# Per-slot amounts of filler, and their pace within a slot, in a convolution and attention kernel on Trainium2

## The chip, the cores and the metric

The kernel runs on one core of one Trainium2 chip. The core has a matrix engine (TensorE, PE in the profile), a vector engine (VectorE, DVE), a scalar engine (ScalarE, ACT), a general one (GpSimd, POOL), and a queue for transfers (SyncE, SP). Each engine works through its own instructions in order; semaphores hold an instruction until what it needs is there. Time is the device time of one execution in microseconds, the median of several.

## What is computed

Eight images of 512 channels by 32 x 32 pixels, all in float32, go through two layers. The first is a group norm, then a block with two bottleneck attentions; the second is a group norm, then a 1 x 1 convolution with a masked and permuted weight matrix. Cut to what matters:

```python
# layer 0, on gn(x): 32 groups
t = silu(bn(conv1x1(gn(x), cv1_w)))              # 512 -> 512
ys = [t[:, :256], t[:, 256:]]
for i in range(2):                               # two blocks
    z = silu(bn(conv3x3(ys[-1], m_cv1_w[i])))    # 256 -> 256
    q, k, v = split(conv1x1(z, m_qkv_w[i]))      # 4 heads of 64
    logits = einsum('bhdi,bhdj->bhij', q, k + r_i) * 64 ** -0.5
    z = einsum('bhij,bhdj->bhdi', softmax(logits), v)
    z = silu(bn(conv1x1(z, m_cv2_w[i])))
    ys.append(ys[-1] + z)
x = x + silu(bn(conv1x1(concat(ys), cv2_w)))     # 1024 -> 512
# layer 1
x = x + conv1x1(gn(x), w_eff)                    # 512 -> 512, w_eff from conv, S, T
```

## The kernel before

**Slots and units.** The attention of one image in one block is a slot; there are 16. In groups of two images the order is (image p, block 0), (p+1, 0), (p, 1), (p+1, 1). Slots are numbered s = 0 to 15, and k below counts groups, so that slot 4k is the first of a group. A slot has four units (`Unit`, line 493): two pairs of heads by two halves of the 1024 queries, pair by pair. The two heads of a pair run side by side in the matrix engine.

**What a unit does.** The keys are cut into eight tiles, taken two at a time in four steps, t = 0, 2, 4, 6. At the start `top` (line 524) transposes the running maxima (tile mt) and VectorE reduces them (nm); `spread` (533) brings the negated maxima back over the partitions (mb). Then in each step, on its engines: `soften` (VectorE adds mb to the stored logits st), `exponent` (ScalarE takes exp of st in place, GpSimd adds it to the sum), `values` (TensorE: po from st and v, for the two tiles before), and `logits` of the **next** unit (TensorE: lg from q and k; ScalarE copies lg to st; VectorE takes the maximum mx). In the step t = 0 come also `finish` and `divide` of the unit before (the denominators den, a reciprocal rb, and q overwritten by po times rb). Four pairs of lists (`pe_turn`, `act_turn`, `in_turn`) fix the order of these instructions on their engines. The order of everything else follows from the order in which the kernel issues it; the framework that compiles the program may move an instruction up where the one ahead of it would wait.

**Filler.** All other work on TensorE is laid between the steps as filler, as Python generators that yield a planned cost in microseconds after each piece (called planner us below). A piece of a 1 x 1 convolution is two matmuls and counts 1.72, a piece of the 3 x 3 convolution (`conv3`, Winograd products) three matmuls and 1.33, a piece of values' projection eight matmuls and 0.89. In the profile each float32 matmul of the program is two instructions.

**What is needed in a slot** is what the next slot's attention wants: `conv3` of the next slot's image (six products of four pieces, 31.9), `project` (q, k and v; per pair of heads four pieces of 1.72 and two of 0.89, 17.3 in sum, planned as 21), and where images come to their second block `conv_m2` (four pieces, planned as 7). After a block-1 slot `conv_m2(1)` of its image is needed too, and then `finishing` puts four items on the background list.

**The background list** (`Background`, line 849) holds work that no attention waits for soon: `First` (normalisation and first convolution of half an image; four groups of two pieces, 13.76 in all), `Second` (the convolution over the concatenation; four groups of four pieces, 27.5) and `Last` (layer 1; four groups of two pieces, 13.76). A group ends in an evacuation: SiLU on ScalarE for First and Second, an addition on VectorE for Last. An item's loads are issued when the item ahead of it begins, and it has a planned time from which it is ready. At the start the list holds eleven First items (the twelfth is held back); `finishing` adds two Second items, the item held back and one Last item, 82.6 in all, and holds another Last item. `take(us)` (line 867) runs pieces up to that amount, to the end of a group, and what it runs over is taken off the next `take`. Where the list is empty it returns, and where the next item isn't ready it returns, or, with `wait=True`, lets planner time pass without work.

**A slot's filler** (`slot_filler`, line 912) is a list of takes in this order: 8 from the list; for a next slot of block 1, conv_m2(0), then 9 from the list; conv3 (after a block-1 slot: 16 pieces of it, then conv_m2(1) and `finishing`, then the rest of it); 7 from the list; project; where the slot after the next is of block 0, the load of its y and the eight VectorE operations that transform it for conv3, timed by the planner's clock from 8.0 on and 3.3 apart. The sum of the planned amounts is `needed`: 68 in slot 0, 84 in slots 4k+1 and 4k+2, 75 in slots 4k+3 and in slots 4k from 4 on. Behind it comes the rest, the share (`SHARE`) less `needed`, from the list; in slot 15 the rest is 70. `total` is the sum of both.

**The pace** is set by `advance` (line 1041). A slot has 40 equal steps, ten a unit. In unit j it is called at 10j + 0.7 (before top), + 1.4 (before spread), + 2 (before the step t = 0), and then after each of the steps at + 4, + 6, + 8 and + 10. It runs filler until the planned amount reaches a goal, the larger of two terms: the share of the slot times `total`, and a term that completes `needed` at a certain share of the slot. The next slot's first logits are those that the fourth unit issues in its step t = 0, right after the call at step 32 (a share of 0.80). When the slot ends, what is left of its filler is run.

**Ahead and behind.** Before slot 0 the first two images are normalised and convolved, the weights of the 3 x 3 convolutions and of layer 1 are prepared, and the first unit's logits are taken among four takes of 6.8 after one of 7. After slot 15 come the last divisions, conv_m2(1) of the last image, its Second items and the last two Last items.

Of the kernel before, what the change touches and what calls it, by code (L numbers as in the profile page):

```python
# [39 lines left out]
def conv_preact_kernel(ctx: ExitStack, tc: tile.TileContext, x, cv1, cv2, mcv1, qkv, mcv2, bn, rw, rh, conv, s_in, t_in, out):  # L40
# [859 lines left out]
    def call(f, *a):  # L900
        f(*a)
        return
        yield

    def finishing(im):


        bg.add(Second(im, 0), Second(im, 1), held.pop(), Last(im, 0))
        held.append(Last(im, 1))
        bg.prepare()  # L910

    def slot_filler(s):

        prev = slots[s - 1] if s else (None, 0)
        nxt = slots[s + 1] if s + 1 < len(slots) else (None, 0)
        todo, needed = [], 0.0

        def add(us, g):
            nonlocal needed
            todo.append((us, g))  # L920
            needed += us

        im, i = nxt
        add(8.0, bg.take(8.0))
        if im and i == 1:
            add(7.0, im.conv_m2(0))
            add(0.0, call(im.transform, 1, 2.0, 3.3))
            add(9.0, bg.take(9.0))
        products = im.conv3(i) if im else iter(())
        if prev[1] == 1:  # L930
            if im:
                add(21.3, (us for _, us in zip(range(16), products)))
            add(7.0, prev[0].conv_m2(1))
            add(0.0, call(lambda: finishing(prev[0])))
        if im:
            add(10.7 if prev[1] == 1 else 32.0, products)
            add(7.0, bg.take(7.0))
        if im:
            add(21.0, im.project(i))
        if s + 2 < len(slots) and slots[s + 2][1] == 0:  # L940
            add(0.0, call(slots[s + 2][0].load_y))
            add(0.0, call(slots[s + 2][0].transform, 0, 8.0, 3.3))
        rest = SHARE - needed if im else 70.0
        if rest > 0:
            todo.append((rest, bg.take(rest, wait=True)))
        total = sum(c for c, _ in todo)
        return needed, total, todo

    SHARE = 103.0


    small_parameters()
# [71 lines left out]
    before = None  # L1024
    for s in range(len(slots)):
        needed, total, todo = slot_filler(s)
        state = {"done": 0.0}

        def filler():
            for us, g in todo:  # L1030
                start = state["done"]
                for cost in g:
                    clock.tick(cost)
                    state["done"] += cost
                    yield

                state["done"] = max(state["done"], start + us)

        fill = filler()

        def advance(share):
            goal = max(share * total, min(1.0, share / 0.74) * needed + 0.1)
            while state["done"] < goal:
                if next(fill, "end") == "end":
                    break

        steps = 4 * (KT + 2)
        for j in range(4):
            u = units[4 * s + j]
            nxt = units[4 * s + j + 1] if 4 * s + j + 1 < len(units) else None  # L1050
            base = j * (KT + 2)

            advance((base + 0.7) / steps)
            u.top()
            clock.tick(0.9)
            advance((base + 1.4) / steps)
            u.spread()
            clock.tick(0.9)
            advance((base + 2) / steps)
            for t in range(0, KT, 2):  # L1060
                if before and t == 0:
                    before.finish()
                    clock.tick(0.9)
                u.soften(t)
                u.soften(t + 1)
                if t:
                    u.exponent(t)

                lag = u if t else before
                if lag:  # L1070
                    lag.values((t - 2) % KT)
                    lag.values((t - 1) % KT)
                    clock.tick(2.0)
                if before and t == 0:
                    before.divide(0)
                    before.divide(1)
                if nxt:
                    nxt.logits(t)
                    nxt.logits(t + 1)
                    clock.tick(2.0)  # L1080

                if not t:
                    u.exponent(t)
                u.exponent(t + 1)
                advance((base + 4 + t) / steps)
            before = u
        for _ in fill:
            pass
# [6 lines left out]
    im = images[NB - 1]  # L1095
# [55 lines left out]
```

## Time and profile before

| what | value |
|---|---|
| median of 3 runs | 3153.09 us (3151.32 to 3154.78) |
| the profiled execution | 3162.82 us, its span 3161.1 us, mean granted TensorE clock 0.996 |
| TensorE busy, matmuls | 3077.0 us, 97% of the span |
| VectorE, ScalarE, GpSimd busy | 2049.9 us (65%), 1721.0 us (54%), 1398.4 us (44%) |
| slot 0 begins (first transposes of its first unit) | 212.3 us |
| slots 1, 2, 3, 4 begin | 398.3, 579.2, 747.0, 926.5 us |
| slots 14 and 15 begin, the last unit begins | 2698.0, 2877.2, 2993.9 us |
| transfers | 399.35 MB, 126 GB/s over the span |

"Busy" is time in which at least one instruction of an engine runs. A line of groups gives the source line, the engine, the operation, tiles out<-in, shapes, a count, then busy time and the mean of one, and the idle time of the engine just before, with what ended it. A line of the windows view gives a stretch in microseconds from the start, its length, the busy time (and count) of PE, PEld (TensorE's weight loads), DVE, ACT and POOL, the granted clock of TensorE as a part of full speed, and the share and rate of the transfers. A line of the timeline gives start, length, engine, line, operation, tiles, shape and count of a run of like instructions, and in brackets the idle time before it and what ended it. A slot is found in the trace by its transposes mt: each unit begins with eight of them.

### The profile page before, as it was taken

The numbers are of one execution on the slowest core, as the hardware profiler recorded it, in microseconds if no ns is written. First come the engines' busy times: TensorE is split into PE (matmuls) and PEld (weight loads), VectorE is DVE, ScalarE is ACT, GpSimd is POOL, SyncE is SP. The second block draws the span as 40 slices with busy tenths as digits, with TensorE's granted clock in tenths as the row PEclk, the third lists the DMA queues.
The fourth block names the chain that finished last, engine by engine and source line by source line (L and its number), as shares of the span: only waits on it lengthen the run. The fifth ranks groups of instructions, "written<-read, shape, count | busy, mean of one in ns | idle before, by whom it ended". The sixth has DMA issues, their size and how long they took to land.

```text
span 3161.1 us, 34185 instructions
## 1 busy us (share of the span) xinstructions
PE 3077.0 (97%) x11668; PEld 1515.3 (48%) x11668; DVE 2049.9 (65%) x2718; ACT 1721.0 (54%) x2349; POOL 1398.4 (44%) x1867
## 2 busy tenths in 40 slices
PE   7999999998999999999999999999999999999999
PEld 3645354454445454455445454454445454453333
DVE  5446577567667576667666676767666676767642
ACT  3245765855655555644656455544656455546621
POOL 2104444546444554455444454445444464444520
PEclk9999999999999999999999999999999999999999
DMA  8852352421233232424233332424233332413356
GB/s 289 292 182 74 130 180 87 153 77 63 88 116 131 79 128 71 149 84 148 84 116 130 114 127 70 153 85 136 91 110 130 120 120 70 150 64 120 120 205 217
DMA packets 142014, 399.35 MB, mean 126 GB/s; under 512 B 13072, under 2 KB 14352, under 8 KB 141840
## 3 DMA queue, kind: packets, MB, share of 16 engines
q1 hardware_dynamic: 141120, 396.94, 36.6%
q8 instruction: 92, 1.51, 0.2%
q14 instruction: 82, 0.67, 0.1%
q10 hardware_dynamic: 720, 0.23, 0.0%
HBM read 317.42 MB, written 79.69 MB: 126 GB/s over the span
## 4 chain that ended last, share of the span: by engine, by line
PE 75%; DVE 4%; ACT 4%; issue 2%; DMA 1%; POOL 1%; SPq 0%; ACTq 0%; DVEq 0%; POOLq 0%
PE cv L175 15%; PE m L313 13%; PE po L562 12%; PE lg L510 12%; PE l L175 7%; PE qk L175 6%; PE v L405 3%; PE m L175 3%; PE den L576 2%; PE mb L539 2%; PE mt L530 1%; ACT st L517 1%; DVE st L544 1%; ACT st L548 1%; DVE mx L522 1%
## 5 line engine op out<-in xcount | busy, mean ns | idle before, releaser
L555 POOL TENSOR_TENSOR sum<-sum,st 128x256 f32<-128x256 f32 x1536 | 1132.0, 771 | 552.1 <-ACT st L548 547.7
L522 DVE TENSOR_TENSOR mx<-mx,lg 128x512 f32<-128x512 f32 x768 | 477.8, 682 | 417.6 <-ACT st L517 417.4
L517 ACT COPY st<-lg 128x512 f32<-128x512 f32 x1024 | 525.0, 597 | 356.1 <-PE lg L510 331.7
L548 ACT ACTIVATE st<-st 128x1024 f32<-128x1024 f32 x512 | 539.1, 1068 | 304.1 <-DVE st L544 302.9
L544 DVE TENSOR_TENSOR st<-st,mb 128x1024 f32<-128x1024 f32 x512 | 604.4, 1215 | 60.2 <-PE mb L539 60.2
L555 POOL TENSOR_TENSOR sum<-st,st 128x256 f32<-128x256 f32 x256 | 185.1, 754 | 788.8 <-ACT st L548 788.8
L313 PE MATMUL m<-plane,w_m 128*128 128x256 f32 x2304 | 528.8, 383 | 4.9 <-ACT cv2s L130 2.7
L562 PE MATMUL po<-st,v 128*64 128x512 f32 x2048 | 497.8, 605 | 18.2 <-ACT st L548 16.2
L510 PE MATMUL lg<-q,k 64*128 64x512 f32 x2048 | 510.9, 617 | 2.9 <-ACT y L130 2.9
L313 PEld LDWEIGHTS m<-plane,w_m 128*128 128x128 f32 x2304 | 426.4, 189 | 129.5 <-issue 45.1
L175 PE MATMUL cv<-y,w_cv 128*128 128x512 f32 x1024 | 464.5, 599 | 7.9 <-ACT cv2s L130 4.6
L510 PEld LDWEIGHTS lg<-q,k 64*128 64x128 f32 x2048 | 177.3, 186 | 328.2 <-issue 267.4
L175 PEld LDWEIGHTS cv<-y,w_cv 128*128 128x128 f32 x1024 | 185.8, 190 | 248.1 <-issue 226.4
L562 PEld LDWEIGHTS po<-st,v 128*64 128x64 f32 x2048 | 128.8, 136 | 323.6 <-issue 237.3
L175 PE MATMUL cv<-x,w_cv 128*128 128x512 f32 x512 | 237.0, 610 | 10.6 <-ACT y L130 3.7
L175 PE MATMUL l<-x,w_l 128*128 128x512 f32 x512 | 236.9, 606 | 7.9 <-DVE mx L522 6.9
L175 PE MATMUL qk<-z,w_qkv 128*128 128x512 f32 x512 | 234.0, 600 | 1.4 <-DVE mx L522 1.4
L583 DVE RECIPROCAL rb<-rb 128x256 f32<-128x256 f32 x128 | 215.5, 1723 | 26.0 <-ACT rb L579 25.8
L531 DVE TENSOR_REDUCE nm<-mt 128x4 f32<-128x512 f32 x128 | 82.3, 684 | 144.7 <-PE mt L530 144.7
L579 ACT COPY rb<-den 128x512 f32<-128x512 f32 x64 | 37.3, 583 | 230.4 <-PE den L576 230.4
L175 PEld LDWEIGHTS cv<-x,w_cv 128*128 128x128 f32 x512 | 95.3, 194 | 132.0 <-issue 109.3
L175 PEld LDWEIGHTS l<-x,w_l 128*128 128x128 f32 x512 | 93.4, 191 | 130.4 <-issue 112.2
(145 smaller groups left out, 2408.8 us busy)
## 6 DMA issues: line engine op xcount, KB each, us to landing
w_m<-w_m SPq DMA_DIRECT2D x96, 768.0 KB, 4.8
w_cv<-in_cv SPq DMA_DIRECT2D x90, 512.0 KB, 3.5
y<-y SPq DMA_DIRECT2D x64, 512.0 KB, 4.8
x<-in_x SPq DMA_DIRECT2D x56, 512.0 KB, 5.2
y<-y SPq DMA_DIRECT2D x64, 256.0 KB, 3.5
k<-r SPq DMA_DIRECT2D x32, 512.0 KB, 3.6
res<-y SPq DMA_DIRECT2D x32, 512.0 KB, 4.0
xr<-in_x SPq DMA_DIRECT2D x32, 512.0 KB, 4.1
```

The costliest lines, as they stand in the source:

```text
L175: nc.tensor.matmul(ps, w, moving, start=(n == 0), stop=(n == len(terms) - 1))
L313: nc.tensor.matmul(ps[:, ts(co, 256)].rearrange("p (t x) -> p t x", x=F), w[:, co, c, dx], u[:, 9 * c : 9 * c + 8, dx : dx + F], start=(j ...
L405: nc.tensor.matmul(ps[:, ts(j, P)], z[:, c, ts(4 * j4 + j, P)], w[:, c, 512 + P * hp : 512 + P * hp + P], start=(c == 0), stop=(c == IT - 1),)
L510: nc.tensor.matmul(lg[h], self.k[r, ts(t, P)], self.q[r, self.hp, ts(self.half, HALF)], start=True, stop=True)
L517: act_turn(nc.scalar.copy(st[:, h], lg[h]))
L522: in_turn(nc.vector.tensor_tensor(self.mx[:, h], so_far[:, h], lg[h], ALU.max))
L531: nc.vector.tensor_reduce(self.nm[:, h], mt, AX.X, ALU.max, negate=True)
L544: in_turn(nc.vector.tensor_tensor(st, st, flat(self.mb), ALU.add))
L548: act_turn(nc.scalar.activation(st, st, AF.Exp))
L555: nc.gpsimd.tensor_tensor(flat(self.acc)[:, part], flat(so_far)[:, part], st[:, part], ALU.add)
L562: nc.tensor.matmul(self.po[HD * h : HD * h + HD], self.v[:, t, ts(h, HD)], self.st[t][:, h], start=(t == 0), stop=(t == KT - 1),)
L583: nc.vector.reciprocal(self.rb[:, r], self.rb[:, r])
```

## The change

The number SHARE, 103 for every slot, becomes a table: 92 in slot 0, 96 in slot 1, 95 in slots 2 and 14, and 103 in the others. In the pace, the share of the slot at which all needed work is to be done goes from 0.74 to 0.80.

```diff
@@ slot_filler
-        rest = SHARE - needed if im else 70.0
+        rest = SHARE.get(s, 103.0) - needed if im else 70.0
         if rest > 0:
             todo.append((rest, bg.take(rest, wait=True)))
         total = sum(c for c, _ in todo)
         return needed, total, todo
 
-    SHARE = 103.0
+
+    SHARE = {0: 92.0, 1: 96.0, 2: 95.0, 14: 95.0}
@@ advance, in the loop over the slots
         def advance(share):
-            goal = max(share * total, min(1.0, share / 0.74) * needed + 0.1)
+            goal = max(share * total, min(1.0, share / 0.8) * needed + 0.1)
             while state["done"] < goal:
                 if next(fill, "end") == "end":
                     break
```

## The prediction

> **What bounds the kernel now.** I read the page first, for the engine that carries the span, then TensorE's share unit by unit (the windows view, cut at the first transpose of each unit), then the order of instructions where a unit runs short.
>
> ```profile
> span 3161.1 us, 34185 instructions
> PE 3077.0 (97%) x11668; PEld 1515.3 (48%) x11668; DVE 2049.9 (65%) x2718; ACT 1721.0 (54%) x2349; POOL 1398.4 (44%) x1867
> PE   7999999998999999999999999999999999999999
> ...
> PE 75%; DVE 4%; ACT 4%; issue 2%; DMA 1%; POOL 1%; SPq 0%; ACTq 0%; DVEq 0%; POOLq 0%
> ```
>
> TensorE is idle for 3161.1 - 3077.0 = 84 us. The change leaves every matmul in place and reorders filler, so it can win or lose only such idle time, and stretches at a low clock. Some 19 us lie ahead of slot 0 and 13 in the last unit and the tail (windows view, 167.20 - 154.36 = 12.8), which it does not touch. Of the rest, these units have most (columns: stretch, length, then busy time of PE, PEld, DVE, ACT, POOL, the clock, DMA):
>
> ```profile
> 349.50:398.20 48.70, 46.54 (x153) 18.98 (x152) 27.51 (x41) 41.13 (x51) 20.49 (x29) 1.00 0.43 147
> 539.90:579.10 39.20, 38.09 (x133) 15.45 (x132) 24.35 (x34) 32.81 (x41) 19.02 (x27) 1.00 0.26 85
> 718.70:746.90 28.20, 20.40 (x92) 7.41 (x90) 25.01 (x31) 16.63 (x26) 19.09 (x26) 1.00 0.08 29
> 747.00:785.90 38.90, 38.26 (x168) 22.22 (x169) 30.13 (x38) 19.27 (x29) 27.25 (x36) 1.00 0.27 87
> 1422.10:1458.70 36.60, 35.37 (x127) 14.28 (x126) 31.95 (x41) 16.60 (x25) 21.97 (x27) 1.00 0.45 158
> 2840.10:2877.10 37.00, 35.77 (x125) 13.91 (x124) 26.13 (x33) 18.00 (x26) 19.25 (x28) 1.00 0.38 131
> 2877.20:2913.60 36.40, 32.33 (x113) 11.96 (x112) 25.87 (x32) 27.18 (x35) 19.48 (x29) 0.95 0.38 132
> ```
>
> Length less PE: last unit of slot 0 2.16, of slot 1 1.11, **of slot 2 7.80**, first of slot 3 0.64, last of slot 6 1.23, last of slot 14 1.23, **first of slot 15 4.07**. The timeline of TensorE shows why (the bracket is idle time before the group):
>
> ```profile
> 724.02 1.99 PE L510 MATMUL lg<-q,k 64*128 64x512 f32 x8
> 728.28 2.02 PE L562 MATMUL po<-st,v 128*64 128x512 f32 x8 [2.28 <-ACT st L548]
> ...
> 735.62 1.08 PE L562 MATMUL po<-st,v 128*64 128x512 f32 x4 [2.38 <-ACT st L548]
> ...
> 740.92 1.08 PE L562 MATMUL po<-st,v 128*64 128x512 f32 x4 [1.29 <-ACT st L548]
> ```
> ```profile
> 1429.44 1.12 PE L175 MATMUL l<-x,w_l 128*128 128x512 f32 x2
> 1431.79 2.02 PE L562 MATMUL po<-st,v 128*64 128x512 f32 x8 [1.23 <-DVE mx L522]
> ```
> ```profile
> 1245.91 1.98 PE L175 MATMUL cv<-y,w_cv 128*128 128x512 f32 x4
> 1248.26 2.02 PE L562 MATMUL po<-st,v 128*64 128x512 f32 x8 [0.37 <-ACT st L548]
> ```
> ```profile
> 2882.53 1.99 PE L510 MATMUL lg<-q,k 64*128 64x512 f32 x8
> 2888.24 3.31 PE L562 MATMUL po<-st,v 128*64 128x512 f32 x8 [3.72 <-ACT st L548]
> ```
>
> Between the logits and the values of a step, ACT must copy the logits and take exponents. With no filler there TensorE idles 2.3 us, with two matmul instructions 1.2, with four 0.4. Slot 2's last unit has no filler at all.
>
> **Why it has none: the planner's sums.** A First item is four groups of 3.44 planner us, 13.76; eleven are on the list, 151.4. Taken before slot 0: 34.4. Slot 0 takes 8+7+35 = 50, slot 1 8+9+7+19 = 43, slot 2 24 before its rest: 151.4, and the rest of 19 finds nothing. The list is filled again in slot 3 after its first 8, and then by 82.6 in each of two slots of four (165 against the 164 taken), so the first 8 of slots 7, 11 and 15 find nothing either. Slots 7 and 11 have the convolution's products at once; slot 15 has only one projection piece, hence 4.07.
>
> **The change part by part.** *Shares.* With 92, 96 and 95 the rests of slots 0 to 2 are 24, 12 and 11. In whole groups, slot 0 gives up 10.3 and slot 1 6.9; slot 2 gets 10.3 and slot 3's first take 6.9; slot 14 gives 6.9 to slot 15's first take. Each sum is conserved, so the tail is the same. *Pace.* Where needed/0.74 exceeds the share (84 needed, slots 4k+1 and 4k+2: 113.5 against 103) the needed work now runs at 105 and ends at step 32 of 40 instead of 29.6. Where 75 is needed (101.4 and now 93.8, against 103) the second term never ruled, and still does not.
>
> (a) Slot 2's last unit now holds 13.8 planner us of filler, but unevenly: the end of the projection and half a group up to step 32, nothing at steps 34 and 36, then 3.4 and 5.2. Two empty steps: the open half group can be pulled into the first (four instructions leave 0.4, two 1.2; 0.8), the second is bare (mean of 2.38 and 1.29: 1.8). 7.8 becomes 2.6: **-5.2**; ends -7.4 (0.4 in all) and -1.9 (the three bare waits, 5.95).
> (b) The last units of slots 1 and 14 lose half their rest and get the same two empty steps: 1.11 and 1.23 become 2.6, **+2.9** in sum. Ends per slot: 0.8 in all (-0.4), or 3.72 + 2.38, the first with the 1.28 us table load on ACT seen at slot 15 (+4.9).
> (c) Slot 15's first unit gets four pieces of 1.72 where it starved; 4.07 becomes about 0.5 (0.64 in slot 3's first unit): **-3.6**; ends -4.1 and 0, if the Last item's normalisation is late.
> (d) Slots 6 and 10: the empty steps of the last unit shrink from three to one, ahead of four instructions: 1.23 to 0.4, **-1.6**; ends -2.5 and +2. Slots 5, 9 and 13 keep one empty step ahead of a Second group, 0.37 as now: 0.
> (e) Slot 0's last two units idle 1.71 and 2.16, with ACT busy 41.13 of 48.70 on SiLU, its tables and normalisation. Their First work thins (26 to 17 in the last unit) and goes where ACT is busy 16.63 of 28.20 and 19.27 of 38.90. Half goes: **-1.9**; ends -3.9 and +1.5.
> (f) Filler visits: twelve instructions at 0.43 us (3.70 to 5.42 us is four more) are 5.16 us, but such a visit takes 5.35 up to the next values, so 0.2 per visit; about four more visits net: **+0.8**, ends 0 and +2.
>
> Costed at nothing: the moved DMAs. First groups carry 512 KB loads of weights (3.5 us to landing) and 256 KB stores (3.5), the Last item two loads (3.5, 3.3) and a store (4.8); SP's queue has room, DMA share 0.08 in slot 2's last unit and 0.38 in slot 15's first. The later projection takes along its 768 KB load (4.2), two k loads (3.6), k's additions on DVE and the q and v copies on ACT. The half for the next unit's heads is 8.7 planner us ahead of the end, so its logits have some 15 us; if that cover went, the wait would be rival 2's. The load of y and eight transform operations for slots 3, 7 and 11 come about 2.4 steps (11 us) later; 8 + 7 x 3.3 = 31 planner us still fit in the last unit, and the next thing late would be the first products.
>
> Sum: -5.2 + 2.9 - 3.6 - 1.6 - 1.9 + 0.8 = **-8.6 us** against the profiled execution (span 3161.1, its own time 3162.82, 9.7 above the median of the runs). I carry the difference to the median: 3153.09 - 8.6 = **3144.5 us**.
>
> **Two rules weighed.** Clock: after the 3.72 us gap the values took 3.31 us in place of 2.02, at a clock of 0.95; after slot 2's 2.28 and 2.38 the clock stayed 1.00. I book no change of it, since one such dip may go at slot 15 and one may come in a new hole. The Trainium skill ("TensorE: Matmul & The Clock Gate", section "Why this matters for your kernels") says to leave no TensorE gaps above about 3 us; by it only slot 15's dip counts and the sum would be -9.9. The skill's "TensorEngine Tiling", section "Key Properties", says that a change of tiling mode drains TensorE. It speaks against spreading filler over more visits, which alternate 128*128 with 64*128 and 128*64; the trace's price for it is (f), and without the rule the sum would be -9.4.
>
> **The rivals.** *1, the holes stay whole:* nothing is pulled forward, and slots 1, 2 and 14 idle the full 3.72 + 2.38 = 6.1. Then (a) is -1.7, (b) +9.9, and the sum +1.9: 3155.0. For it: all the bare steps above. Against: in slot 6 two instructions of a later piece moved up into the hole. *2, slower:* the projection now ends right before the next slot's first logits; if k's addition stands in DVE behind a reciprocal pair, a division, a maximum and a softening (3.36 + 0.69 + 1.28 + 2.35 = 7.7 us) the logits wait. In eight slots at 2.0 us each that is +16: 3160.5. It decides from (8.6 + 6.3)/8 = 1.9 us a slot. Against it: the 15 us of cover, and only 2.9 us idle ahead of all logits now. *3, more is gained:* the holes fill (0.8 in all), the dip at slot 15 goes, slot 0 idles no more: -7.0 - 0.7 - 3.6 - 1.3 - 1.6 - 3.9 + 0.8 = -17.3, and half way from the forecast 3140. *4, it does not do what it says:* the moved groups are not ready where they are put (planner waits without work), so only (c) comes: 3149.5.
>
> **How the numbers follow.** A measurement of this kernel tells about 0.2%, 6.3 us, from no change: faster is below 3146.8, slower above 3159.4. Forecast 50% (3140.5 to 3148.5; four fifths of it faster), rival 1 18% (same, a little of it slower), rival 2 8% (two thirds slower), rival 3 19% (faster), rival 4 5% (same). Faster 0.40 + 0.19 = 0.59 and 0.01 of rival 4, so 0.60; slower 0.04 + 0.05 = 0.09 and a little for what I do not see, 0.11; same 0.29. The range leaves out rival 2's far half and rival 3's: 3137 to 3158; the likeliest case's own is 3140.5 to 3148.5.
>
> **What would show it.** Filler in slot 2's last unit, which grows from 28 to about 35 us with idle below 3.5; no gap of 3 us at the start of slot 15; two gaps of 0.5 to 2.5 in the last units of slots 1, 2 and 14; slot 0 shorter by some 11 us, slot 3 longer by 7. I am wrong if those holes cost 5 us each, if logits wait after step 32, or if units that I left alone change by more than 1 us.

## The result

The changed kernel takes 3185.53 us where the kernel before takes 3152.28 us beside it: a ratio of 1.0102, with a 95% interval of 1.0087 to 1.0117. In a later run, listed below, the ratio was 1.0081 (1.0066 to 1.0097). The change is slower by some 0.8 to 1.0%; the forecast was 0.27% faster.

The profiled execution has a span of 3182.5 us, 21.4 above that of before. (That one lay 10 us above its median, so the traces show about two thirds of the difference of the medians. A second trace of each, taken later, differs by 27.6 us.) From the page of the changed kernel, span and busy times:

```profile
span 3182.5 us, 34189 instructions
...
PE 3089.4 (97%) x11668; PEld 1524.0 (48%) x11668; DVE 2040.0 (64%) x2718; ACT 1731.7 (54%) x2355; POOL 1391.9 (44%) x1867
...
PE 80%; ACT 5%; DVE 5%; issue 2%; DMA 2%; POOL 1%; ACTq 0%; SPq 0%; DVEq 0%; POOLq 0%
```

The same 11668 matmul instructions are busy for 12.4 us longer (3077.0 before), which is the clock's doing: its granted mean went from 0.996 to 0.992, and 0.4% of the span is 12.7 us. And TensorE is idle for 93.1 us, 9.0 more. The two make up the 21.4. (The end of the program hides a part: from the last unit on TensorE idles 7.9 us here, but 12.8 in the first trace of before and 8.5 in its second. Ahead of the last unit idle time grew by 11 to 14 us.) Where they lie, in the windows view of the changed kernel, again unit by unit (last of slot 0, first of 1, last of 1, first and last of 2, first of 3, first and last of 6, first and last of 14, first of 15; columns as before):

```profile
338.40:389.60 51.20, 47.12 (x150) 19.19 (x149) 29.23 (x46) 38.28 (x49) 20.42 (x29) 0.97 0.44 149
389.60:441.70 52.10, 47.45 (x155) 20.51 (x154) 37.70 (x58) 39.22 (x48) 20.66 (x28) 0.93 0.63 201
534.10:573.70 39.60, 35.94 (x134) 14.70 (x134) 23.97 (x30) 26.63 (x35) 19.40 (x28) 0.96 0.17 58
573.80:634.60 60.80, 48.88 (x149) 21.57 (x148) 36.76 (x55) 39.45 (x50) 22.70 (x29) 0.89 0.51 168
725.30:768.30 43.00, 37.81 (x149) 16.32 (x148) 31.08 (x36) 27.17 (x38) 23.22 (x28) 0.96 0.24 79
768.40:809.80 41.40, 41.40 (x184) 24.93 (x183) 25.50 (x32) 24.23 (x33) 22.48 (x30) 1.00 0.39 135
1304.10:1352.10 48.00, 43.65 (x151) 18.81 (x150) 36.12 (x47) 33.00 (x42) 20.71 (x27) 1.00 0.56 187
1443.10:1482.30 39.20, 38.81 (x148) 16.93 (x147) 32.32 (x41) 17.77 (x27) 22.00 (x27) 1.00 0.43 150
2723.20:2774.70 51.50, 46.51 (x151) 19.88 (x150) 35.99 (x47) 32.99 (x42) 20.96 (x28) 0.93 0.53 173
2865.70:2902.10 36.40, 34.11 (x130) 13.93 (x129) 24.93 (x31) 17.98 (x27) 19.38 (x28) 0.95 0.25 83
2902.20:2941.10 38.90, 37.50 (x129) 14.54 (x128) 27.99 (x34) 28.57 (x36) 19.96 (x28) 1.00 0.49 172
```

The worst is a unit that the forecast did not price at all: the **first unit of slot 2**, with 60.80 - 48.88 = 11.9 us idle at a mean clock of 0.89. Its line in the kernel before was this, and under it two lines of TensorE's timeline there:

```profile
579.20:627.50 48.30, 46.17 (x157) 20.42 (x156) 30.61 (x38) 42.29 (x52) 19.01 (x26) 0.96 0.53 174
```
```profile
589.08 3.70 PE L175 MATMUL cv<-x,w_cv 128*128 128x512 f32 x8
...
609.73 8.83 PE L175 MATMUL cv<-x,w_cv 128*128 128x512 f32 x16 [2.13 <-ACT m2s L130]
```

The timeline of the changed kernel there, TensorE, then VectorE, then ScalarE:

```profile
578.99 1.97 PE L539 MATMUL mb<-ident,nm 128*128 128x128 f32 x8 [2.48 <-DVE nm L531]
...
586.13 1.99 PE L510 MATMUL lg<-q,k 64*128 64x512 f32 x8
593.93 0.56 PE L146 MATMUL gm_a<-mv_a,gmat 128*128 128x4 f32 x2 [5.81 <-DVE mv_a L144]
594.35 6.24 PE L175 MATMUL cv<-x,w_cv 128*128 128x512 f32 x8
...
630.42 4.43 PE L313 MATMUL m<-plane,w_m 128*128 128x256 f32 x12 [3.62 <-DVE plane L282]
```
```profile
572.68 1.29 DVE L139 BATCH_NORM_STATS2 st_a<-x 128x6 f32<-128x512 f32 x2 [3.48 <-DMA x<-in_x]
577.06 1.29 DVE L139 BATCH_NORM_STATS2 st_a<-x 128x6 f32<-128x512 f32 x2 [3.09 <-DMA x<-in_x]
578.26 1.27 DVE L531 TENSOR_REDUCE nm<-mt 128x4 f32<-128x512 f32 x2
...
582.20 2.46 DVE L139 BATCH_NORM_STATS2 st_a<-x 128x6 f32<-128x512 f32 x4
...
585.70 3.36 DVE L583 RECIPROCAL rb<-rb 128x256 f32<-128x256 f32 x2
...
592.76 0.69 DVE L522 TENSOR_TENSOR mx<-st,lg 128x512 f32<-128x512 f32 x1 [2.50 <-ACT st L517]
593.37 0.42 DVE L144 BATCH_NORM_AGGREGATE mv_a<-st_a 128x2 f32<-128x12 f32 x4
```
```profile
590.74 1.52 ACT L165 ACTIVATE x<-x,go_a,gr_a 128x512 f32<-128x512 f32 x2 [1.83 <-DMA x<-in_x]
592.17 0.56 ACT L517 COPY st<-lg 128x512 f32<-128x512 f32 x1
```

This is the group norm of the last image. Its statistics wait on VectorE for loads of x, and the unit's own reduction nm stands behind them in VectorE's order; then the group norm's matmul gm stands in TensorE's order and waits 5.81 us for their summary, mv_a. The statistics themselves are done at 584.7. The summary stands in VectorE's order behind the unit's reciprocals, division and maxima, and one of these maxima waits 2.50 us for a copy of logits, which ScalarE has behind two normalisations that wait 1.83 us for a load of x. The eight matmul instructions after gm take 6.24 us; eight of the same kind took 3.70 us in the kernel before. The third wait, 3.62 us, is for a plane of the 3 x 3 convolution's input.

### The profile page after: what moved, and what is told of

Read it like the earlier page. It is cut to its first block, busy times and chain, and to the rows that moved or that the text cites. A ratio compares the mean times of both kernels' runs of the same rounds, so it can differ in the third digit from the quotient of the medians.

```text
span 3182.5 us, 34189 instructions
## 1 busy us (share of the span) xinstructions
PE 3089.4 (97%) x11668; PEld 1524.0 (48%) x11668; DVE 2040.0 (64%) x2718; ACT 1731.7 (54%) x2355; POOL 1391.9 (44%) x1867
## 4 chain that ended last, share of the span: by engine, by line
PE 80%; ACT 5%; DVE 5%; issue 2%; DMA 2%; POOL 1%; ACTq 0%; SPq 0%; DVEq 0%; POOLq 0%
PE cv L175 16%; PE m L313 14%; PE lg L510 13%; PE po L562 12%; PE qk L175 7%; PE l L175 7%; PE v L405 3%; PE m L175 2%; PE mb L539 2%; PE den L576 2%; PE mt L530 2%; DMA x<-in_x 1%; DVE st L544 1%; ACT st L517 1%; ACT st L548 1%
## 5 line engine op out<-in xcount | busy, mean ns | idle before, releaser
L510 PEld LDWEIGHTS lg<-q,k 64*128 64x128 f32 x2048 | 180.9, 187 | 325.6 <-issue 269.2
L531 DVE TENSOR_REDUCE nm<-mt 128x4 f32<-128x512 f32 x128 | 82.4, 685 | 170.9 <-PE mt L530 170.8
```

Source lines behind the costliest of these rows:

```text
L510: nc.tensor.matmul(lg[h], self.k[r, ts(t, P)], self.q[r, self.hp, ts(self.half, HALF)], start=True, stop=True)
L531: nc.vector.tensor_reduce(self.nm[:, h], mt, AX.X, ALU.max, negate=True)
```

## The experiments

Two theories stood at first: A, that the shares of slots 0 to 2 lose, because moved First items bring statistics, loads and normalisations along; B, that the pace loses, because needed work comes too late.

**The parts, each alone.**

```diff
 shares_012:  SHARE = {0: 92.0, 1: 96.0, 2: 95.0}, pace 0.74
 share_14:    SHARE = {14: 95.0}, pace 0.74
-pace_only:   share / 0.74
+pace_only:   share / 0.8, SHARE 103 for all
```

> The kernel before with the shares of slots 0, 1 and 2 alone set to 92, 96 and 95; the pace stays 0.74 and slot 14 stays at 103. Theory A (the moved First items bring their x loads, statistics, group norm matmuls and normalisations into the first units of slots 1 and 2, and TensorE's stalls there lower its clock): most of the whole change's +33 us is here, +20 to +33 us, with idle of over 8 us in slot 2's first unit. Theory B (the pace of 0.80 puts the needed work too late): -8 to 0 us, slot 2's last unit filled and no new stall in its first unit. Theory C (each part is harmless, only both together lose): within 6 us of before.

> The kernel before with slot 14's share alone set to 95. All theories: the idle at the start of slot 15 goes (4.1 us to about 1), the last unit of slot 14 idles some 1 to 3 us more: -4 to +2 us.

> The kernel before with the pace of 0.80 alone. Theory A: within 5 us of before, the last units of slots 6 and 10 idle 0.4 us in place of 1.2, slot 2's last unit still has no filler of the background list and idles 6 to 8 us. Theory B: +20 us or more, with waits of the next slot's logits or of the 3 x 3 convolution's products.

> The kernel before, unchanged, for a second trace: its profiled execution of 3162.82 us lies 10 us above its median. If that was chance of the clock, this one lies nearer to 3152 us with fewer stretches at half clock and the same idle time in the slots, within 3 us.

Measured, as ratios to the kernel before: shares_012 1.0026 (1.0017 to 1.0036), share_14 0.9999 (0.9985 to 1.0013), pace_only 1.0056 (1.0039 to 1.0073). Neither theory alone: both parts lose, the pace more. before_again has a span of 3161.8 us, idle for 82.4 us, so the first trace was no odd one in its waits; that chance of the clock had made it long was not borne out. share_14 moved idle time more than it removed it: the first unit of slot 15 idles 1.41 us in place of 4.07, the last of slot 14 3.13 in place of 1.23. The shares' loss shows in the first unit of slot 2, as A said (idle 55.80 - 48.38 = 7.4 us, clock 0.94, in the windows view of shares_012). It has the first two of the three waits, 2.48 and 4.95 us, and not the third:

```profile
565.30:621.10 55.80, 48.38 (x161) 21.58 (x160) 36.72 (x55) 39.80 (x50) 20.01 (x26) 0.94 0.56 187
```

The pace's, in its trace, lies mostly in slot 1, 192.5 us long against 180.9, where the list holds First items and ScalarE is about as busy as VectorE (126.6 and 122.8 us of the slot). The timeline of pace_only has a wait there and slow matmuls behind it (six take 2.74 us elsewhere in that trace):

```profile
435.06 1.99 PE L510 MATMUL lg<-q,k 64*128 64x512 f32 x8
440.13 5.49 PE L175 MATMUL cv<-x,w_cv 128*128 128x512 f32 x6 [3.09 <-ACT y L130]
```

The third wait of slot 2's first unit, for a plane, is in this trace too, 2.19 us: it comes with the pace and not with the shares.

**ScalarE or the statistics?** Two kernels without SiLU, so without the exchange of tables (1.28 us each), and the pace kept out of slots 0 to 2.

```diff
-nc.scalar.activation(dst, src, AF.Silu, bias=..., scale=...)      # light_before, light_after
+nc.scalar.activation(dst, src, AF.Identity, bias=..., scale=...)
-goal = max(share * total, min(1.0, share / 0.74) * needed + 0.1)   # pace_from_3
+goal = max(share * total, min(1.0, share / (0.8 if s > 2 else 0.74)) * needed + 0.1)
-clock.at(12.0, gn0.mean); clock.at(16.0, gn0.var); normed = now + 16.0   # after_late_mean
+clock.at(20.0, gn0.mean); clock.at(24.0, gn0.var); normed = now + 24.0
```

> The kernel before with the scaled and shifted identity in place of every SiLU, so that the values differ and ScalarE needs no tables exchanged between SiLU and exponent (left out: the SiLU itself). Read as the base for the next run. Theory A2 (the loss is ScalarE's: where First items and conv_m2 fill a slot, ScalarE with its 1.28 us table loads is the bound, and its order puts normalisations that wait for x ahead of the copies of logits): 3130 to 3150 us. Rival C (the loss is in VectorE's and TensorE's order: statistics that wait for x, group norm matmuls): near 3150 us.

> The changed kernel with the same identity in place of every SiLU. Theory A2: without the table loads the two kernels lie within 8 us of each other. Rival C: it stays 20 to 33 us above the run before it, with the 5.8 us wait of the group norm's matmul in slot 2's first unit.

> The kernel before with the pace of 0.80 from slot 3 on and 0.74 in slots 0 to 2. If the pace costs only where the list holds First items (slots 1 and 2), this lies within 5 us of before and slot 1 is again 181 us long; if it costs in every slot of 84 needed, it stays 10 us or more above.

> The changed kernel with the group norm's two small matmuls of a First image 8 planner us later (20 and 24 in place of 12 and 16). Theory C: the 5.8 us wait in slot 2's first unit goes and with it 6 to 15 us of the loss, clock included: 3170 to 3179 us where before is 3152. Theory A2: at most 6 us of it goes, since ScalarE stays as full.

light_before is at 0.9969 of the kernel before (0.9953 to 0.9985), light_after at 0.9996 (0.9984 to 1.0009). The two are 0.27% apart, some 8.5 us (2 to 15 us by their intervals), where the full kernels are 0.8 to 1.0% apart: without the tables the change loses less, but it still loses. The first unit of slot 2 is hardly better for it. It idles 10.0 us, and light_after still waits for the group norm (its timeline):

```profile
567.78 1.25 PE L539 MATMUL mb<-ident,nm 128*128 128x128 f32 x8 [1.70 <-DVE nm L531]
...
579.89 0.56 PE L146 MATMUL gm_a<-mv_a,gmat 128*128 128x4 f32 x2 [4.49 <-DVE mv_a L144]
580.31 6.39 PE L175 MATMUL cv<-x,w_cv 128*128 128x512 f32 x8
```

Its two other waits are there as well (1.70 us above, and 3.80 us for the plane). What shrank lies elsewhere. Slot 1 is 12.3 us shorter in light_after than in light_before, where the full change made it 3.3 us longer; but light_before has waits of its own there, and its slot 1 takes 187.6 us where before takes 180.9, so the pair doesn't tell how much of this is the change. The first units of slots 6, 10 and 14, which lose with the full change, lose nothing here: they idle 2.64, 0.87 and 2.23 us in light_after and 2.55, 3.31 and 2.51 in light_before. So C's "20 to 33" is missed, A2's "within 8 us" can't be told from what was measured, and light_before's own time, 3148.5 us, fits both.

pace_from_3 is at 1.0024 (1.0014 to 1.0034): about 0.3% of the pace's 0.56% lies in slots 0 to 2 and about 0.2% later, some 8 us, between the two answers that I had set (within 5 us, or 10 and more). In its trace slots 6 and 10 are 2.7 and 4.5 us longer. In the first unit of slot 6 TensorE waits behind a SiLU that ScalarE reaches late, having first run two normalisations of a Last item, and the matmuls after the wait are slow again, 5.40 us for eight (timeline of pace_from_3):

```profile
1317.68 1.99 PE L510 MATMUL lg<-q,k 64*128 64x512 f32 x8
1323.46 5.40 PE L175 MATMUL l<-x,w_l 128*128 128x512 f32 x8 [3.80 <-ACT cv2s L130]
```

The kernel before had a wait of 2.48 us in this unit and no slow stretch behind it. after_late_mean gave 1.0097 (1.0076 to 1.0117) and settles nothing: its edit also touched the images ahead of slot 0, which cost 9 us there, while the 5.8 us wait did shrink to 2.4.

**Only the last image's statistics.**

```diff
+late = 8.0 if self.im.n == NB - 1 else 0.0                          # after_late_7
-clock.at(12.0, gn0.mean); clock.at(16.0, gn0.var); normed = now + 16.0
+clock.at(12.0 + late, gn0.mean); clock.at(16.0 + late, gn0.var); normed = now + 16.0 + late
 # after_early_7: Background.prepare runs early() of the last image's First
 # when the second half of image 5 begins (slot 1), not when image 6 does (slot 2)
+more = [(self.first + 2, "early")] if items[first] is First(images[6], 0) else []
-for j, stage in ((self.first + 1, "early"), ...):
+for j, stage in (*more, (self.first + 1, "early"), ...):
 # share_0: the kernel before, SHARE = {0: 92.0};  share_1: SHARE = {1: 96.0}
```

> The changed kernel with the last image's loads of x for its statistics, the statistics and the two group norm matmuls one item earlier, in slot 1 in place of the start of slot 2. Theory C (they stall VectorE and TensorE at the start of slot 2): idle of slot 2's first unit falls from 11.9 to below 5 us, the stretches at half clock in slot 2 from 17 to below 9 us, and the ratio to before from 1.010 to 1.005 or less. Theory A2 (ScalarE is full there in any case): the ratio stays above 1.007.

> The changed kernel with only the last image's two group norm matmuls 8 planner us later; loads and statistics stay. Theory C: the 5.8 us wait shrinks to 2.4 us as in the run with all images later, ratio to before 1.006 to 1.009, and nothing moves ahead of slot 2. Theory A2: 1.009 to 1.011.

> The kernel before with slot 0's share alone at 92. Three groups of First work move from slot 0 to slot 2; image 7's statistics fall into the last unit of slot 1 and slot 2's last unit gets 8.6 planner us of filler. If the loss of the three shares is in where image 7's statistics fall, this is within 5 us of before or up to 6 us faster.

> The kernel before with slot 1's share alone at 96. Two groups move from slot 1 to slot 2; image 7's statistics begin where they do before and slot 2's last unit gets 5.2 planner us. Within 5 us of before or up to 6 us faster; a loss of more than 6 us would say that the moved groups themselves cost, wherever the statistics fall.

after_early_7 is at 1.0045 (1.0028 to 1.0063), after_late_7 at 1.0059 (1.0042 to 1.0075): with nothing changed but when one image's statistics are taken, about half of the loss goes, and with nothing changed but when its two small matmuls, and the normalisations behind them, are run, 0.2 to 0.4% (the wait ahead of gm is 2.71 us there). In after_early_7 the first unit of slot 2 is 14.6 us shorter than in the changed kernel and at full clock, while slot 1, where the statistics now fall, is 2.5 us longer. Of the three waits the first two are gone from slot 2; the third, for the plane, is still 2.46 us. Its windows view:

```profile
574.50:620.70 46.20, 42.31 (x146) 17.55 (x145) 31.39 (x38) 40.74 (x51) 20.82 (x27) 1.00 0.53 175
```

share_0 is at 1.0003 (0.9994 to 1.0012), share_1 at 1.0007 (0.9998 to 1.0017). Each fills slot 2's last unit in part, and neither gains from it. In share_1 that unit idles 4.9 us, but the last unit of slot 1 4.5 in place of 1.1. In share_0 the idle time of slot 2's last unit falls from 7.8 to 32.20 - 29.61 = 2.6 us. That is the number reckoned for the full change, by luck: here it is one wait of 1.23 us for the exponents and one of 1.36 at the next slot's transposes, not two empty steps (windows view of share_0):

```profile
717.60:749.80 32.20, 29.61 (x116) 11.86 (x114) 27.29 (x34) 26.00 (x34) 18.35 (x24) 1.00 0.27 96
```

But slots 0 to 3 together are no shorter (719.5 us against 714.1 and, in the second trace of before, 715.4; some 1.7 us of it are four matmul instructions that before runs ahead of slot 0): the group norm of the last image now waits at the end of slot 1 (2.64 us ahead of its first matmul) and at the start of slot 2.

**What was open: the rest, and the sum.**

```diff
 # shares_early_7: shares_012 with the statistics as in after_early_7, pace 0.74
 # after_again: the changed kernel, unchanged
```

> The three shares (92, 96, 95) at the old pace of 0.74, with the last image's statistics one item earlier. If the loss of the shares (0.26% in the run of them alone) is where these statistics fall, it goes: a ratio to before of 1.000 or less, down to 0.997 (slot 2's last unit no longer starves, 8 us); then what is left of the loss with the statistics earlier (0.45%) is the pace's. If the moved groups cost of themselves, it stays at 1.002 to 1.003.

> The changed kernel, unchanged, beside the others: a second trace and a ratio from this chip. If the parts add up (shares 0.26%, pace 0.56%, slot 14 nothing) it is 1.008; the first measurement gave 1.010. The waits in slot 2's first unit are the same three, within 1 us each.

shares_early_7 is at 1.0006 (0.9996 to 1.0016): without the pace, and with the statistics out of slot 2, nothing of the loss is left in the ratio, and nothing is gained either. The traces, one execution each, don't place this as clearly: slot 4 begins at 930.6 us here, at 932.9 in shares_012 and at 926.5 and 928.5 in the two of before, since most of what slot 2 wins slot 1 loses. With the whole change they do: slot 4 begins at 950.3 us in the changed kernel and at 936.3 in after_early_7. after_again is at 1.0081, and the parts measured alone multiply to the same (1.0026 x 1.0056 x 0.9999). Its waits in slot 2's first unit are the same three (3.22, 5.67 and 4.36 us). No version that computes the same result beats the kernel before.

## Why the prediction was wrong

**What held: the planner's sums and the priced idle times, roughly.** By the count of First items' matmul instructions, slot 0 gave up 20 (24 forecast) and slot 1 16 (16), slot 2 took 32 (24) and slot 3 8 (16). The last unit of slot 14 idles 2.29 us (2.6 forecast), of slot 1 3.66 (2.6), of slots 6 and 10 0.39 (0.4), the first of slot 15 1.40 (0.5). Two were poorer. Slot 2's last unit still idles 5.19 us (2.6 forecast, 5.95 the bound): its two empty steps waited three times, the second one twice (timeline of the changed kernel):

```profile
740.99 2.02 PE L562 MATMUL po<-st,v 128*64 128x512 f32 x8 [1.91 <-ACT st L548]
742.94 1.99 PE L510 MATMUL lg<-q,k 64*128 64x512 f32 x8
746.39 1.08 PE L562 MATMUL po<-st,v 128*64 128x512 f32 x4 [1.46 <-ACT st L548]
749.28 1.61 PE L562 MATMUL po<-st,v 128*64 128x512 f32 x4 [1.81 <-ACT st L548]
```

And (e) gained nothing: slot 0's last two units idle 4.1 us (3.9 before). All the terms that I named come to (5.19 - 7.80) + (3.66 + 2.29 - 2.34) + (1.40 - 4.07) - 1.7 + 0.2 = -3.2 us of idle time, against -9.4 forecast. The rule on tiling modes does show in the traces: where the next matmul instruction has another tile shape (`128*128`, `64*128`, `128*64`), one of 512 columns takes 0.52 us from start to start in place of 0.43, and one of 256 columns 0.31 in place of 0.22. At some 0.09 us a change, (f) was small, as forecast; how many visits the change adds was not counted.

**The step that failed first: "Costed at nothing: the moved DMAs".** I listed what a moved First group loads and stores, and left out what a First *item* triggers when it begins: four loads of the next image's x, eight statistics on VectorE, two matmuls in TensorE's order at a planned delay, normalisations on ScalarE. With 17 planner us taken from slots 0 and 1, the item that triggers the last image's statistics moved into the start of slot 2, where a unit begins and conv_m2's SiLUs run (before, they ran in the third unit of slot 1 and gm in the fourth, with no wait ahead of it). That cost the first two waits, 2.48 and 5.81 us, and the slow matmuls behind them. after_early_7 shows it: with the same filler and the statistics moved, both waits go and with them 0.4 to 0.6%; after_late_7 and the ratio of shares_early_7 agree. The third wait, 3.62 us, is the pace's: it is in pace_only, and not in shares_012.

**The second: "I book no change" of the clock.** It is over half of the loss in the trace, 12.4 of 21.4 us. One dip was to go and one to come; in slots 0 to 3 the stretches at half clock grew instead, from 10 to 34 us, and half of these 24 us more is lost; the first unit of slot 2 alone fell to a mean of 0.89.

**The third: (d), which priced the pace in the last units of its slots alone.** The pace also thins the filler of the first ones. The first units of slots 6, 10 and 14 idle 4.35, 4.56 and 4.99 us (3.35, 3.11 and 2.83 before), and those of slots 1 and 2 more. The first unit of slot 6 in the kernel before, in its windows view:

```profile
1280.80:1329.40 48.60, 45.25 (x159) 19.90 (x158) 35.81 (x47) 32.71 (x42) 22.75 (x28) 1.00 0.56 184
```

pace_only prices all of it at 0.56%, pace_from_3 the later slots at 0.24%. That the wait is for ScalarE, and longer because ScalarE comes to the SiLU late, is read from the releasers in these units (a SiLU ends the longest wait of each) and from the light pair, where these units lose nothing. The pace alone without SiLU was not tried, so in slots 1 and 2 ScalarE's part stays open.

**Rival 2** named the right sign and the wrong place: no trace has a wait of more than 0.2 us ahead of the next slot's logits after step 32. TensorE is idle for 0.0 us ahead of all logits in the changed kernel's page, 2.9 before.

The gain itself, slot 2's starved unit, was real but small and unspendable: share_0 removed 5 of the 7.8 us there, and slots 0 to 3 came out no shorter. The sign of being wrong that the prediction named last, units left alone that change by more than 1 us, is the one that came.

## What to carry to other kernels

When filler is moved, follow every item to the moment at which it *begins*, and move with it all that this triggers on other engines' queues; two matmuls of four columns, standing in order behind other engines' queues and a load, cost 5.8 us of waiting and 2.5 us of slow matmuls here, where a whole unit without filler idled 7.8. Price each new wait of the matrix engine above some 2 us with the slow matmuls that may follow it. And when a pace fills the end of a slot, price its beginning too: here the last units of slots 6 and 10 won 0.8 us each and the first ones lost 1.0 and 1.5.

## What the runs showed of the hardware

Waits of TensorE of 2 to 6 us were often paid for again by slow matmuls behind them, but not each time. In the changed kernel eight instructions after the 5.81 us wait took 6.24 us in place of 3.70, and the transposes after a wait of 2.48 us took 1.97 in place of 1.04. In the kernel before, sixteen instructions after a wait of 2.13 us took 8.83 us where sixteen take 7.13 elsewhere, yet a wait of 2.48 us in slot 6 had nothing of the kind behind it, nor had the same wait of 2.13 us in the second trace of before, nor one of 3.09 us in slot 6 of the changed kernel. Counted over all sixteen traces, from slot 0 up to the last unit, a stretch at half clock began during a wait, or within 3.5 us after it, in 25 of 53 waits of 2.0 to 2.5 us, 17 of 25 of 2.5 to 3.0, 11 of 16 of 3.0 to 3.5, and all 25 longer ones. The Trainium skill ("TensorE: Matmul & The Clock Gate", section "Why this matters for your kernels") puts the limit at idle gaps of about 3 us. Here about half of the gaps of 2.0 to 2.5 us were followed by a slow stretch too, so the measurement sets a lower and less certain mark than the page.
